# One GpSimd instruction for du * B of two states, and two states in PSUM less often in layer 1

## The chip, the cores and the metric

The kernel runs on one core of one Trainium2 chip. The time is device microseconds from start to end of one execution; the median of three runs before the change is 11,260.47 us (11,260.01 to 11,280.23).

## The reference

Four images of 64 x 64 pixels and 96 channels go through four layers. Layers 0 and 1 are selective scans (layer 0 on the pixels with 192 inner channels, layer 1 on a two-dimensional Fourier transform with 384 inner channels and 64 x 33 positions); layers 2 and 3 are linear attention and a quantized feed-forward block. The change is in the scan that layers 0 and 1 share. Each runs over four directions, with 16 states per channel:

```python
def step(hst, inputs):
    ul, dl, bl, cl = inputs
    dA = jnp.exp(dl[..., None] * A)
    hst = hst * dA + (dl * ul)[..., None] * bl[:, :, None, :]
    y = jnp.einsum('bkdn,bkn->bkd', hst, cl)
    return (hst, y)
```

For every position l, channel d and state n: h = h * exp(delta * A) + (delta * u) * B, and y sums h * C over the 16 states.

## The kernel before

**Phases, segments, steps.** The work has six phases: two for layer 0 (two images each, 64 channels of either side by side on the 128 partitions) and four for layer 1 (an image each). A phase runs through four directions, each cut into segments along the sequence: eight of 512 positions in layer 0, five of 512, 512, 384, 384 and 320 in layer 1. That gives 64 segments in layer 0 and 80 in layer 1. A segment has 12 steps: for each group q of four states (q = 0 to 3), the three chunks c of channels (128 rows each). So there are 768 steps in layer 0 and 960 in layer 1, and each step makes four scans, of states 0 to 3 of its group.

**What a step does on each engine.**
- DVE: four scans along the positions (`scan`, L710). The factor `exp(delta * A)` of states 0 and 1 lies in SBUF (`ax`) and their addend B*du in PSUM, put there by PE's transposes (`transposed`, L678). For states 2 and 3 it is the other way round: the factor lies in PSUM (`ay`), and the addend in the SBUF tile `h`.
- POOL (GpSimd): `front_b` (L700) makes that addend, du * B, for states 2 and 3 of the next step, two instructions into `h[:, 1]` and `h[:, 2]`. `multiply` (L744, L747) saves the last column of the previous step's states and multiplies them by C in place, for the states whose result is in `h`.
- States that are "kept" leave their result in PSUM (`kept_at`). DVE multiplies it by C (`multiply_kept`, L728), ACT saves its last column (`keep_state`, L735). State 0 is kept in every step; state 3 too in some steps, chosen by `self.kept`: every second step in layer 0 (`cfg.KI` is 1), every fourth in layer 1 (`cfg.KI` is 2). In a step with one kept state POOL multiplies three states, in a step with two it multiplies two.
- PE: transposes for the next step, and the sum over states by accumulating transposes into `acc` (`add_rest` and `add_kept`, both by `accumulate`, L757).
- ACT: the exponentials (L682), `make_bx` (L646) and copies.

**Order.** The order on each engine is written out by hand in the loop over `steps`. In step i, PE first accumulates the states of step i-2 (`add_rest(older)`); POOL does `multiply(before)` of step i-1 and then `front_b(nxt)` for step i+1; DVE does scans 0 to 3 of step i with its kept product behind scan 0 and, where state 3 is kept, behind scan 3. The tile `h` has three buffers, so `front_b` for step i+1 writes where step i-2 stood and waits until PE has accumulated that one. PSUM has three banks for the operands of the scans, used in rotation. Other work (projections, transforms, the layers after) runs as generators, `slot` by `slot`, between the steps; GpSimd's part of it are the transposing copies (L335), du itself (L604) and small additions (L1352, L1356).

Of the kernel before, what the change touches and what calls it, by code (L numbers as in the profile page):

```python
# [11 lines left out]
ALU = mybir.AluOpType  # L12
# [10 lines left out]
C, P = 3, 128  # L23
# [7 lines left out]
class Cfg:  # L31
# [5 lines left out]
    def __init__(self, pre, NI, KI, NR, nat, R, parts, rows, segs, eps):  # L37
        self.pre = pre
        self.NI, self.PI, self.KI = NI, P // NI, KI
        self.DI = C * self.PI  # L40
        self.NR, self.L, self.nat = NR, NR * 64, nat
        self.R, self.M = R, R + 2 * NST
        self.parts = parts
        self.rows = [(sum(rows[:i]), n) for i, n in enumerate(rows)]
        self.segs = [(sum(segs[:i]), n) for i, n in enumerate(segs)]
        self.eps = eps
# [466 lines left out]
class Step:  # L513


    def __init__(self, z, q, c):
        self.z, self.q, self.c = z, q, c
        self.nm = f"{z.nm}_{q}_{c}"
        self.kept = (0, 3) if (C * q + c) % (2 * z.cfg.KI) == 1 else (0,)
        self.hk = {}  # L520
        self.px, self.ay = {}, {}


def scans(tc, ctx, phases, ident):
# [8 lines left out]
    nc = tc.nc  # L533
# [161 lines left out]
    def front_b(st):  # L695

        S = st.z.S
        st.h = sp.tile([P, 3, SM], F32, name=f"h_{st.nm}", tag="h", bufs=3)
        for j in range(2):
            nc.gpsimd.tensor_tensor(  # L700
                st.h[:, 1 + j, :S], st.z.du[:, st.c, :S], st.z.b[st.q][:, j, :S], ALU.mult
            )

    def scan(st, j):
        z = st.z
# [93 lines left out]
    with tc.manual_schedule(engines=IN_ORDER):  # L799
# [4 lines left out]
        st = steps[0]  # L804
        for j in range(2):
            transposed(st, j)
        front_x(st)
        front_b(st)
        before = older = None
        more, pgen, pwants, at, due = Pieces(segs[0], 1, 4), none, None, 0, 0.0  # L810
# [32 lines left out]
        for i, st in enumerate(steps):  # L843
            z, q, c, S = st.z, st.q, st.c, st.z.S
# [42 lines left out]
            if nxt:  # L887
                front_b(nxt)
# [734 lines left out]
```

## Time and profile before

The profiled execution took 11,260.07 us, of which 11,258.3 are the span from the first to the last instruction. The mean granted TensorE clock is 0.898. The scan loop runs from 216 to 10,873 us.

| phase | from, us | length, us | steps | us per step |
|---|---|---|---|---|
| layer 0, images 0 and 1 | 216 | 2471 | 384 | 6.44 |
| layer 0, images 2 and 3 | 2687 | 2443 | 384 | 6.36 |
| layer 1, image 0 | 5130 | 1452 | 240 | 6.05 |
| layer 1, image 1 | 6582 | 1415 | 240 | 5.90 |
| layer 1, image 2 | 7997 | 1434 | 240 | 5.97 |
| layer 1, image 3 | 9431 | 1443 | 240 | 6.01 |

The starts are those of each phase's first scan in the timeline. The page's table gives, by engine, busy time and share of the span; rows by line and shape give count, busy time, mean duration, and the idle time of the engine just before, with what ended it. A mean duration of a POOL row includes an overlap of some tens of ns with the next instruction, which start-to-start times in the timeline do not.

### The profile page before, as it was taken

To read this page: it belongs to the slowest core of one execution; us is meant where nothing else is said; L and a number is where in the kernel's file an instruction comes from. 1 tells how busy PE (TensorE), PEld (TensorE's weight loads), DVE (VectorE), ACT (ScalarE), POOL (GpSimd) and SP (SyncE) were. 2 spreads that over 40 slices of the span, in tenths; PEclk is the share of its full clock that TensorE was granted. 3 is DMA by queue.
4 is the path that set the end of the run, shared out by engine and by line. 5 is a ranking of instruction groups with operands and counts; after the bars stand their busy time and mean duration, and the time that the engine had idled before them with its cause. 6 is when DMAs were issued, how large, how long until landed. Compare 5 with 4: busy or idle time off the path is not lost. (4 is left out here: it accounts for less than half of the span.)

```text
span 11258.3 us, 163664 instructions
## 1 busy us (share of the span) xinstructions
PE 9023.4 (80%) x54944; PEld 6618.2 (59%) x54944; DVE 9756.0 (87%) x10419; ACT 9354.2 (83%) x19456; POOL 9614.9 (85%) x7464
## 2 busy tenths in 40 slices
PE   6678788777888888888888888887788777887775
PEld 2555555555667666656665665655556555655554
DVE  6889999889999998999888787988988889789864
ACT  3779999998898998998778788879888888778853
POOL 2999999888998998999789798988989889889860
PEclk8889999888998998999889899998899888899887
DMA  4655554555665556555554444542244322542242
GB/s 146 146 131 128 133 131 120 153 158 143 163 162 134 137 138 144 133 144 161 154 141 131 128 135 137 172 118 92 96 138 143 102 92 98 157 125 96 82 131 40
DMA packets 1205139, 1466.87 MB, mean 130 GB/s; under 512 B 480839, under 2 KB 1017295, under 8 KB 1145799
## 3 DMA queue, kind: packets, MB, share of 16 engines
q1 hardware_dynamic: 1204295, 1456.40, 47.7%
q8 instruction: 434, 7.11, 0.3%
q14 instruction: 410, 3.36, 0.1%
HBM read 1219.66 MB, written 236.50 MB: 129 GB/s over the span
## 5 line engine op out<-in xcount | busy, mean ns | idle before, releaser
L747 POOL TENSOR_TENSOR h_l<-h_l,bc_l 128x1536 f32<-128x1536 f32 (+2 forms) x1728 | 4784.4, 2769 | 192.1 <-DVE h_l L710 73.1
L700 POOL TENSOR_TENSOR h_l<-du_l,bc_l 128x512 f32<-128x512 f32 (+2 forms) x3456 | 3970.4, 1172 | 620.1 <-PE acc_l L757 581.1
L646 ACT ACTIVATE bx_l<-dut_l,bt_l 128x192 f32<-128x192 f32 (+2 forms) x6272 | 2754.6, 499 | 0.3
L757 PE MATMUL acc_l<-ident,h_l 128*128 128x128 f32 (+1 forms) x16656 | 2430.6, 299 | 243.5 <-POOL h_l L747 242.1
L757 PEld LDWEIGHTS acc_l<-ident,h_l 128*128 128x128 f32 (+1 forms) x16656 | 2130.9, 154 | 836.8 <-POOL h_l L747 384.9
L682 ACT ACTIVATE ax_l<-delta_l,l_alog 128x512 f32<-128x512 f32 (+2 forms) x3456 | 2140.7, 667 | 0.0
L710 DVE TENSOR_TENSOR_SCAN h_l<-b_l,state_l,h_l 128x512 f32<-128x512 f32 (+2 forms) x1388 | 1507.6, 1109 | 123.1 <-ACT b_l L682 104.5
L678 PE MATMUL b_l<-ident,bx_l 128*128 128x128 f32 (+1 forms) x6886 | 1215.4, 295 | 210.2 <-DVE h_l L710 203.2
L678 PEld LDWEIGHTS b_l<-ident,bx_l 128*128 128x128 f32 (+1 forms) x6886 | 854.6, 149 | 816.6 <-DVE h_l L710 464.4
L682 ACT ACTIVATE b_l<-delta_l,l_alog 128x512 f32<-128x512 f32 (+2 forms) x1970 | 1232.6, 626 | 117.2 <-DVE h_l L710 49.4
L710 DVE TENSOR_TENSOR_SCAN b_l<-ax_l,state_l,b_l 128x512 f32<-128x512 f32 (+2 forms) x853 | 967.5, 1134 | 254.8 <-PE b_l L678 253.6
L678 PE MATMUL ab_l<-ident,bx_l 128*128 128x128 f32 x5312 | 896.1, 298 | 223.1 <-DVE h_l L710 213.2
L710 DVE TENSOR_TENSOR_SCAN h_l<-ab_l,state_l,h_l 128x512 f32<-128x512 f32 x803 | 992.7, 1261 | 83.2 <-ACT ab_l L682 48.8
L682 ACT ACTIVATE ab_l<-delta_l,l_alog 128x512 f32<-128x512 f32 x1326 | 912.8, 688 | 152.3 <-DVE h_l L710 81.4
L757 PE MATMUL acc_l<-ident,k_l 128*128 128x128 f32 x4760 | 785.8, 293 | 294.8 <-DVE k_l L728 281.6
L710 DVE TENSOR_TENSOR_SCAN h_l<-ax_l,state_l,b_l 128x512 f32<-128x512 f32 (+2 forms) x853 | 963.2, 1129 | 65.0 <-PE b_l L678 62.7
L678 PEld LDWEIGHTS ab_l<-ident,bx_l 128*128 128x128 f32 x5312 | 654.2, 151 | 583.4 <-DVE h_l L710 414.9
L728 DVE TENSOR_TENSOR k_l<-b_l,bc_l 128x512 f32<-128x512 f32 (+2 forms) x1344 | 832.2, 619 | 47.2 <-DMA bc_l<-l_xd_l 1.0
L297 PE MATMUL pc_l<-pad_l,l_dg 128*128 128x512 f32 (+2 forms) x1656 | 788.1, 564 | 59.5 <-ACT uh_l L275 46.8
L757 PE MATMUL acc_l<-ident,hk_l 128*128 128x128 f32 x3628 | 591.8, 297 | 293.7 <-DVE hk_l L728 280.8
L757 PEld LDWEIGHTS acc_l<-ident,k_l 128*128 128x128 f32 x4760 | 582.8, 150 | 390.7 <-DVE k_l L728 317.9
L710 DVE TENSOR_TENSOR_SCAN ab_l<-ax_l,state_l,ab_l 128x512 f32<-128x512 f32 x496 | 631.9, 1274 | 114.5 <-PE ab_l L678 113.8
(252 smaller groups left out, 14452.2 us busy)
## 6 DMA issues: line engine op xcount, KB each, us to landing
bc_l<-l_xd_l SPq DMA_DIRECT2D x640, 512.0 KB
bc_l<-l_xd_l SPq DMA_DIRECT2D x512, 256.0 KB
bc_l<-l_xd_l SPq DMA_DIRECT2D x128, 1024.0 KB
bc_l<-l_xd_l SPq DMA_DIRECT2D x128, 768.0 KB
us_l<-l_u SPq DMA_DIRECT2D x96, 768.0 KB
l_y<-y_l SPq DMA_DIRECT2D x288, 256.0 KB
yt_l<-l_y SPq DMA_DIRECT2D x264, 192.0 KB
yt_l<-l_y SPq DMA_DIRECT2D x128, 384.0 KB
```

What stands on the lines that cost most here:

```text
L297: nc.tensor.matmul(pc[:, : n * 64].rearrange("p (r w) -> p r w", w=64), diag[:, t, :], pad[:, r - p0 + dy : r - p0 + dy + n, dx : dx + 64] ...
L646: nc.scalar.activation(t[:n, b, :, ch], z.dut[:n, b, :, ch], AF.Copy, scale=z.bt[:n, b, m : m + 1])
L678: nc.tensor.transpose(pb[:, t : t + n], st.z.bx[st.q, j][:n, b, st.c], ident[:n, :n])
L682: nc.scalar.activation(out, z.delta[:, st.c, : z.S], AF.Exp, scale=z.blk.A[:, st.c, z.k, n : n + 1])
L700: nc.gpsimd.tensor_tensor(st.h[:, 1 + j, :S], st.z.du[:, st.c, :S], st.z.b[st.q][:, j, :S], ALU.mult)
L710: nc.vector.tensor_tensor_scan(h[:, ::step], a[:, ::step], b[:, ::step], 0.0 if z.first else z.state[st.c][:, n : n + 1], ALU.mult, ALU.add,)
L728: nc.vector.tensor_tensor(hk[:, : z.S], kept_at(st, j), z.c[st.q][:, j, : z.S], ALU.mult)
L747: nc.gpsimd.tensor_tensor(h, h, z.c[st.q][:, 1 : 1 + m, : z.S], ALU.mult)
L757: nc.tensor.matmul(z.acc[st.c][:m, b, :], hc[:, t : t + m], ident, start=(first and b == 0), stop=(last and b == 0), is_transpose=True,)
```

## The change

Two edits. In `front_b` the loop over the two states becomes one `tensor_tensor` over a 2 x S pattern: B of both states is the first operand, and du of the chunk, repeated over the two states by a stride of 0, the second. The values are the same. In `Step`, layer 1 (where `cfg.KI` is 2) keeps state 3 in PSUM in every sixth step of a segment, steps 1 and 7 of 12, where it was steps 1, 5 and 9. Layer 0's rule stays at every second step.

```diff
-        self.kept = (0, 3) if (C * q + c) % (2 * z.cfg.KI) == 1 else (0,)
+        self.kept = (0, 3) if (C * q + c) % (2 if z.cfg.KI == 1 else 6) == 1 else (0,)
...
-        for j in range(2):
-            nc.gpsimd.tensor_tensor(
-                st.h[:, 1 + j, :S], st.z.du[:, st.c, :S], st.z.b[st.q][:, j, :S], ALU.mult
-            )
+        nc.gpsimd.tensor_tensor(
+            st.h[:, 1:, :S],
+            st.z.b[st.q][:, :, :S],
+            st.z.du[:, st.c : st.c + 1, :S].to_broadcast([P, 2, S]),
+            ALU.mult,
+        )
```

## The prediction

> **What bounds the kernel now.** The page's table of engines comes first: no engine is full, four are near it.
>
> ```profile
> span 11258.3 us, 163664 instructions
> ...
> PE 9023.4 (80%) x54944; PEld 6618.2 (59%) x54944; DVE 9756.0 (87%) x10419; ACT 9354.2 (83%) x19456; POOL 9614.9 (85%) x7464
> ```
>
> The chain of waits does not help here: it adds up to some 5% of the span and starts with the last product at 10,873 us, so it covers only the tail. The scan loop before it has to be read by stages. From the timeline I took where each of the six phases' first scan starts, and asked for busy time between these points. Columns: stretch, its length, then busy us and count of PE, PE's weight loads, DVE, ACT, POOL, then clock and DMA.
>
> ```profile
> 216.00:2687.00 2471.00, 1898.48 (x10843) 1350.67 (x10844) 2250.66 (x2148) 2201.16 (x4702) 2311.68 (x1711) 0.91 0.54 136
> 2687.00:5130.00 2443.00, 2025.92 (x12859) 1562.59 (x12857) 2271.86 (x2202) 2220.51 (x4767) 2260.70 (x1658) 0.92 0.59 146
> 5130.00:6582.00 1452.00, 1271.21 (x7802) 946.20 (x7802) 1201.78 (x1348) 1145.53 (x2236) 1238.03 (x1010) 0.90 0.49 142
> 7997.00:9431.00 1434.00, 1142.77 (x7224) 842.74 (x7223) 1283.02 (x1479) 1221.44 (x2514) 1263.63 (x1014) 0.89 0.38 113
> ```
>
> POOL is the fullest engine in the first phase (2311.68/2471 = 94%), DVE in the second (93%), PE in layer 1's first image (88%, its ends modelled), DVE in its third (89%). POOL and DVE lie within 3% of each other in all of them. In equal slices, 560 to 1700 us has POOL at 97% and hardly a wait in it; that is the only stretch where one engine is plainly the bound.
>
> Who waits for whom, over the whole run (engine, instruction, releaser: us, times, longest):
>
> ```profile
> POOL h_l L700 <- PE acc_l L757: 581.1, 336, 7.7
> DVE b_l L710 <- PE b_l L678: 313.6, 254, 6.5
> PE acc_l L757 <- POOL h_l L747: 242.1, 167, 9.2
> DVE h_l L710 <- POOL h_l L700: 54.8, 50, 8.4
> ```
>
> The four lines close a ring. PE's accumulation of step i-2 (add_rest) waits for POOL's product; behind it in PE's queue stand the transposes that DVE's next scans need; and POOL's du * B waits for the same accumulation to release the buffer h. POOL itself waits for PE in 336 of 1728 steps, so in those POOL is ahead and a shorter POOL instruction buys nothing there.
>
> **What the Trainium skill says.** "GPSIMD Engine Reference", section 3.1 (Elementwise), puts a GpSimd tensor_tensor at about 2.6 cycles per element plus a dispatch per instruction. The trace agrees in kind: from the rows below, (3454-2366)/512 = 2.125 ns an element and 2366-1024*2.125 = 190 ns fixed. "Perfetto Trace Analysis", section GPSIMD Engine Instruction, advises start-to-start spacing and not durations; here that matters, see below. "SBUF — State Buffer", section Who interferes with whom, says that a DVE instruction with two SBUF inputs blocks against a GpSimd one that reads SBUF. All four scans and L728 have one operand in PSUM, before and after, and the 128x512 scans take 1259 to 1274 ns whether they write PSUM or SBUF; so I cost a longer POOL instruction at no contention.
>
> ```profile
> L700 POOL TENSOR_TENSOR h_l<-du_l,bc_l 128x512 f32<-128x512 f32 x2304 | 2892.8, 1279 | 309.9 <-PE acc_l L757 293.1 <-issue 14.5 <-POOL h_l L747 1.4
> L747 POOL TENSOR_TENSOR h_l<-h_l,bc_l 128x1536 f32<-128x1536 f32 x672 | 2320.8, 3454 | 81.5 <-DVE h_l L710 33.6 <-DVE qb L1174 3.2
> L747 POOL TENSOR_TENSOR h_l<-h_l,bc_l 128x1024 f32<-128x1024 f32 x480 | 1135.8, 2366 | 39.5 <-DVE h_l L710 6.9
> ```
>
> **The change part by part.** *Merging L700.* By durations a pair costs 2*1279 = 2558 and one instruction of 1024 elements 2366: 192 ns less. But consecutive POOL instructions overlap, as POOL's timeline shows:
>
> ```profile
> 5156.19 2.53 POOL L700 TENSOR_TENSOR h_l<-du_l,bc_l 128x512 f32<-128x512 f32 x2
> 5158.64 0.21 POOL L744 COPY state_l<-h_l 128x3 f32<-128x3 f32 x1
> 5158.93 3.45 POOL L747 TENSOR_TENSOR h_l<-h_l,bc_l 128x1536 f32<-128x1536 f32 x1
> 5162.34 2.50 POOL L700 TENSOR_TENSOR h_l<-du_l,bc_l 128x512 f32<-128x512 f32 x2
> 5164.79 0.18 POOL L744 COPY state_l<-h_l 128x2 f32<-128x2 f32 x1
> 5165.05 2.36 POOL L747 TENSOR_TENSOR h_l<-h_l,bc_l 128x1024 f32<-128x1024 f32 x1
> 5167.37 2.51 POOL L700 TENSOR_TENSOR h_l<-du_l,bc_l 128x512 f32<-128x512 f32 x2
> ```
>
> Start to start the pair takes 5158.64-5156.19 = 2.45 and the 1024-wide product 5167.37-5165.05 = 2.32. The mean over all places without a gap is 2.455 against 2.321 (512), 1.906 against 1.775 (384), 1.637 against 1.505 (320): 0.133 us a step. Layer 0 has 768 steps: 102 us; layer 1 has 960: 128 us. Unknown is the stride-0 operand. L1352, which has one, takes 922 ns for 384 elements and L1356 beside it without one 916, so no penalty; both are shorter than the 1004 of L700 at 384, but both read 16-bit data. Bounds for one merged instruction: 2.455 (nothing gained, loss excluded since two passes do the same) and, if the stride-0 operand were the reason for 922, about 0.19+1024*(0.922-0.19)/384 = 2.14. I take 2.32.
>
> *Layer 1's kept steps.* Two states in PSUM happen in 2 of 12 steps of a segment in place of 3: with 80 segments, 80 steps change. In these POOL multiplies 3 states in place of 2. Start to start that is 3.408-2.321 = 1.087 (512), 2.590-1.775 = 0.815 (384), 2.184-1.505 = 0.679 (320). The five segments of a pass (512, 512, 384, 384, 320) sum to 4.48, times 16 passes: POOL +72 us. DVE loses the L728 of state 3. In gapless DVE steps of the timeline one with it lasts 6.16 and one without 5.43 at 512; 4.87 and 4.28 at 384; 4.12 and 3.57 at 320: 0.73, 0.59, 0.55, sum 3.19, times 16: DVE -51 us. ACT loses 80 state copies (L735) of 0.147 at most, 12 us. PE's matmuls keep their number. The PSUM bank of state 3 is free one L728 sooner.
>
> So POOL: -102 in layer 0, -128+72 = -56 in layer 1. DVE: -51, all in layer 1.
>
> *The wait that is added.* Scan 2 needs half of du * B and scan 3 the other; now scan 2 needs the whole. Behind it on DVE stand scan 3 and the next step's scans, behind those PE's transposes. I paired the k-th two L700 with the k-th four scans of the timeline: the first half ends 3.5 us before scan 2 in the median, yet in 161 of 1728 steps scan 2 starts before or less than 0.14 us after the second half ends. Counted up to 0.1 us after it, the shortfalls add up to 120 us: 44 in layer 0, 76 in layer 1. They come in 57 clusters of neighbouring steps; the largest of each, which is what DVE loses if it only shifts once per cluster, add up to 51. POOL arrives 0.133 us sooner for each step since its last idle moment, about 4 steps (some 430 idle moments in 1728 steps), 0.5 us; mean shortfall is 0.79. So I take 20 us of delay, of which half is caught up in DVE's later waits for PE: +10.
>
> *What of the savings reaches the end.* Phase 1: the 560 to 1700 stretch holds 1140/6.435 = 177 steps, POOL-bound: 177*0.133 = 24. The other 207 steps save 27; PE or DVE wait for POOL in part of them; a third: 9. Phase 2: PE waits for POOL's product there 8.8 us and DVE 3.3 in all; of 51 saved I take 6; DVE is late next. Layer 1: POOL -14 and DVE -13 an image, about 1% of each; when both partners of the ring shrink, PE and ACT (82% and 83% busy over its four images) are next, so I take 70% of the smaller: 9 an image, 36. Sum: -24-9-6-36+10 = -65. The profiled execution's own time is 11260.07, the median 11260.47: the sum gives 11,195 against either.
>
> **The rivals.** *POOL is the bound throughout*: all 102+56 = 158 us arrive, 11,102. For: POOL has the largest share in two of the six phases and lies within 3% of the largest in the others, and PE waits 242 us for its products. Against: the 581 us that POOL waits. *Hidden*: POOL's gain only lengthens its waits for PE, and scan 2's delays eat what DVE gives up, -51+51: 11,260, within 22. For: phase 2's few waits on POOL. Against: the 97% stretch, where nothing can hide it. *Slower*: scan 2 is the place; its shortfalls pass in full, +120, against 33 in phase 1 and DVE's 51: +36, 11,296. The longer run of steps between relieved ones in layer 1 (five in place of three, each with POOL at 3.41+2.32+0.26 = 5.99 against DVE's 5.43 at 512) feeds it: POOL falls behind by 2.8 us there in place of 3*(6.12-5.43) = 2.1. It decides from (33+51)/120 = 70% of the shortfalls on. Against: DVE waits for L700 only 50 times now.
>
> **How the numbers follow.** Below 0.2%, 22 us, a measurement of this kernel can't tell a gain from none. Forecast, a part arrives: 0.50. All arrives: 0.20. Hidden: 0.14. Slower: 0.16. Faster is 0.70 and a little of the hidden case: 0.71; same 0.14; slower 0.15. The range goes from the all-arrives case, with a little for a merged instruction under 2.32, 11,090, to within the slower case, 11,282.
>
> **What would show it.** L700 must appear 1728 times, 2.36 us at 1024 elements; POOL busy near 9614.9-158 = 9457, DVE near 9705. The first phase should shorten by about 33 us, the second by under 15, each image by about 9 less its share of the delays. If DVE's waits for L700 grow from 54.8 to well above 100 us, the slower rival is at work; if L700 lasts 2.5, merging gave nothing; if phase 2 shortens by 40 or more, POOL was the bound where I took DVE.

## The result, and the profile after

The changed kernel takes 11,227.00 us in the median of five runs (11,204.68 to 11,235.58), beside 11,274.52 us for the kernel before (five runs): the ratio is 0.9955, with a 95% interval of 0.9944 to 0.9965. That is 51 us of 11,274.52 by the ratio, where the forecast of 11,195 meant 65. The profiled execution took 11,227.0 us, 33 less than the one of before.

The page of the changed kernel, its span and its table of engines:

```profile
span 11225.2 us, 160774 instructions
...
PE 9045.2 (81%) x54944; PEld 6633.9 (59%) x54944; DVE 9704.5 (86%) x10339; ACT 9343.7 (83%) x19392; POOL 9443.0 (84%) x5736
```

POOL has 9614.9 - 9443.0 = 172 us less to do (forecast 158) and DVE 51 less (forecast 51), and 1728 instructions are gone from POOL. The span is 33 us shorter. So the work went away as it should, and most of the time did not follow.

POOL's two rows of 1024 elements, by line and shape: du * B of two states with its stride-0 operand (L699), and the product of two states with C without one (L749; two lines were added above it).

```profile
L699 POOL TENSOR_TENSOR h_l<-bc_l,du_l 128x1024 f32<-128x1024 f32 x1152 | 2724.8, 2365 | 338.9 <-PE acc_l L759 319.8 <-issue 9.6 <-DVE h_l L712 6.1
L749 POOL TENSOR_TENSOR h_l<-h_l,bc_l 128x1024 f32<-128x1024 f32 x448 | 1059.2, 2364 | 35.9 <-DVE h_l L712 5.1
```

They last the same to 1 ns: the stride-0 operand costs nothing. Start to start, as POOL's timeline has it:

```profile
5164.26 2.37 POOL L749 TENSOR_TENSOR h_l<-h_l,bc_l 128x1024 f32<-128x1024 f32 x1
5166.58 2.39 POOL L699 TENSOR_TENSOR h_l<-bc_l,du_l 128x1024 f32<-128x1024 f32 x1
5168.90 0.19 POOL L746 COPY state_l<-h_l 128x3 f32<-128x3 f32 x1
```

Over all places without a gap the merged instruction takes 2.312 us where the pair took 2.455; 1.764 for 1.906 at 384 columns; 1.495 for 1.637 at 320. That is 0.142 us a step, where 0.133 was forecast.

Busy time by phase in the changed kernel (the same four phases, columns as before):

```profile
217.00:2678.00 2461.00, 1894.58 (x10844) 1344.80 (x10845) 2247.64 (x2148) 2201.61 (x4702) 2258.66 (x1329) 0.90 0.55 136
2678.00:5114.00 2436.00, 2033.30 (x12853) 1568.98 (x12852) 2271.26 (x2202) 2220.27 (x4767) 2207.42 (x1273) 0.92 0.60 146
5114.00:6567.00 1453.00, 1279.17 (x7809) 949.43 (x7807) 1190.88 (x1329) 1144.34 (x2221) 1222.32 (x771) 0.89 0.49 142
7974.00:9404.00 1430.00, 1154.86 (x7215) 855.44 (x7213) 1269.85 (x1458) 1217.30 (x2497) 1245.72 (x774) 0.89 0.38 114
```

By the first scans of the phases in the two timelines, the phases changed by -10.2, -6.8, +0.4, -8.2, -3.1 and -7.4 us, -35 in all. That is less than the 51 of the ratio, mostly because the profiled execution of the kernel before (11,260.07 us) was as fast as the fastest of its five. Phases of the same code differ between the traces of this document by some 5 us in layer 0 and by up to 10 in an image of layer 1, so single phases are known no better. POOL fell by 53 in each of the first two phases (2311.68 to 2258.66, 2260.70 to 2207.42) and got a fifth and an eighth of that back as time.

Who waits for whom:

```profile
POOL h_l L699 <- PE acc_l L759: 617.3, 367, 7.2
DVE b_l L712 <- PE b_l L678: 305.5, 252, 5.0
POOL state_l L746 <- DVE h_l L712: 270.4, 209, 10.7
PE acc_l L759 <- POOL h_l L749: 171.1, 135, 9.8
DVE h_l L712 <- POOL h_l L699: 80.0, 86, 10.1
```

These lines show where the rest went. POOL's waits for PE rose from 581.1 to 617.3 and those for DVE, ahead of the state copy, from 205.5 to 270.4: 101 us that POOL now spends waiting. PE waits less for POOL's products (242.1 to 171.1), but DVE's largest wait, for PE's transposes, nearly stays (313.6 to 305.5; the profile lists the same wait under other tile names too, and all of them add up to 578.9 before and 566.5 after), and DVE waits for du * B 86 times in place of 50.

### The profile page after: what moved, and what is told of

The parts are those of the page before. It is cut to its first block, busy times and chain, and to the rows that moved or that the text cites. A ratio compares the mean times of both kernels' runs of the same rounds, so it can differ in the third digit from the quotient of the medians.

```text
span 11225.2 us, 160774 instructions
## 1 busy us (share of the span) xinstructions
PE 9045.2 (81%) x54944; PEld 6633.9 (59%) x54944; DVE 9704.5 (86%) x10339; ACT 9343.7 (83%) x19392; POOL 9443.0 (84%) x5736
## 5 line engine op out<-in xcount | busy, mean ns | idle before, releaser
L749 POOL TENSOR_TENSOR h_l<-h_l,bc_l 128x1536 f32<-128x1536 f32 (+2 forms) x1728 | 4853.3, 2809 | 208.1 <-DVE h_l L712 64.8
L699 POOL TENSOR_TENSOR h_l<-bc_l,du_l 128x1024 f32<-128x1024 f32 (+2 forms) x1728 | 3718.5, 2152 | 669.2 <-PE acc_l L759 617.3
L759 PEld LDWEIGHTS acc_l<-ident,h_l 128*128 128x128 f32 (+1 forms) x16928 | 2184.2, 155 | 760.0 <-issue 343.0
L759 PE MATMUL acc_l<-ident,h_l 128*128 128x128 f32 (+1 forms) x16928 | 2483.6, 300 | 172.8 <-POOL h_l L749 171.1
L712 DVE TENSOR_TENSOR_SCAN h_l<-ab_l,state_l,h_l 128x512 f32<-128x512 f32 x849 | 1048.9, 1262 | 95.9 <-ACT ab_l L682 49.0
L759 PE MATMUL acc_l<-ident,k_l 128*128 128x128 f32 (+1 forms) x4580 | 759.7, 293 | 283.3 <-DVE k_l L730 270.3
L730 DVE TENSOR_TENSOR k_l<-b_l,bc_l 128x512 f32<-128x512 f32 (+2 forms) x1291 | 800.8, 620 | 44.3
L759 PEld LDWEIGHTS acc_l<-ident,k_l 128*128 128x128 f32 (+1 forms) x4580 | 560.2, 150 | 377.3 <-DVE k_l L730 304.6
```

What stands on the lines that cost most here:

```text
L699: nc.gpsimd.tensor_tensor(st.h[:, 1:, :S], st.z.b[st.q][:, :, :S], st.z.du[:, st.c : st.c + 1, :S].to_broadcast([P, 2, S]), ALU.mult,)
L712: nc.vector.tensor_tensor_scan(h[:, ::step], a[:, ::step], b[:, ::step], 0.0 if z.first else z.state[st.c][:, n : n + 1], ALU.mult, ALU.add,)
L730: nc.vector.tensor_tensor(hk[:, : z.S], kept_at(st, j), z.c[st.q][:, j, : z.S], ALU.mult)
L749: nc.gpsimd.tensor_tensor(h, h, z.c[st.q][:, 1 : 1 + m, : z.S], ALU.mult)
L759: nc.tensor.matmul(z.acc[st.c][:m, b, :], hc[:, t : t + m], ident, start=(first and b == 0), stop=(last and b == 0), is_transpose=True,)
```

## The experiments

Each ratio is against the kernel before on the same chip, with its 95% interval.

**The two edits apart.** The merge alone:

```diff
-        self.kept = (0, 3) if (C * q + c) % (2 if z.cfg.KI == 1 else 6) == 1 else (0,)
+        self.kept = (0, 3) if (C * q + c) % (2 * z.cfg.KI) == 1 else (0,)
```

> The merge alone; layer 1 keeps state 3 every fourth step as before. My theory (both parts bring a share): the merge gives layer 0's whole gain, 17 us by the phase starts of the two traces, and of layer 1 some 10, so ratio near 0.9975 (-28 us). Rival A, the merge does it all: ratio 0.9955. Rival B, the gain is DVE's relief in layer 1 and the merge is hidden by the wait it adds: ratio 0.999 or more.

Measured: 0.9968 (0.9957 to 0.9979), -36 us. POOL's busy time is 9373.0, 242 us less than before. In its trace DVE waits 15 us more for du * B than the 54.8 of before:

```profile
DVE h_l L712 <- POOL h_l L699: 70.0, 63, 10.4
```

So some of what POOL saves is waited for at scan 2.

The kept rule alone, the first hunk of the change's diff, with the pair of instructions as before:

> The kept rule alone (two of 12 steps in layer 1 have two states in PSUM), du * B in two instructions. My theory: DVE loses 51 us, POOL gains 72 in layer 1; about -10 us, ratio 0.999, layer 0 unchanged. Rival A (POOL is the bound of layer 1): slower by 20 to 70 us, ratio 1.002 to 1.006. Rival B (DVE is the bound of layer 1): faster by 30 to 50, ratio 0.996.

Measured: 1.0005 (0.9996 to 1.0013). DVE's busy time fell to 9713.3, 43 less, POOL's rose to 9678.6, 64 more, and the time stood still. So the kept rule on its own brings nothing that can be measured; the merge brings most of the gain, and may bring all of it, since its interval and the change's (0.9944 to 0.9965) overlap.

**The kept rule carried further**, in the changed kernel:

```diff
-        ... % (2 if z.cfg.KI == 1 else 6) == 1
+        ... % (2 if z.cfg.KI == 1 else 12) == 1
```

> The changed kernel with layer 1 keeping state 3 in one step of twelve (step 1 alone): POOL +72 and DVE -51 us against the change, the same again as the change's own second edit. Theory: the exchange of POOL for DVE time is neutral over a wide range, ratio 0.9955 within 0.0015. Rival: layer 1 is tipped to POOL, +20 to +50 us, ratio 0.9975 to 1.000. Rival: DVE is the bound of layer 1, -20 or more, ratio 0.9935.

Measured: 0.9967 (0.9954 to 0.9979). With three, two or one kept step of twelve the merged kernel stands at 0.9968, 0.9955 and 0.9967: no difference is shown. The exchange of some 50 us of DVE for some 70 of POOL is neutral over that range, as far as intervals of some 14 us to either side can tell.

**The added wait alone.** The kernel before with its two instructions in the other order:

```diff
-        for j in range(2):
+        for j in (1, 0):
             nc.gpsimd.tensor_tensor(
```

> The kernel before with the two du * B instructions in the other order, the second state first: POOL's work is unchanged, but scan 2 now waits for both, as it does after the merge. It prices the added wait alone. The prediction's +10 us, at most +20 (before its catching up): ratio 1.001 to 1.002. The slower rival: the 120 us of shortfalls pass in the main, ratio 1.007 to 1.011. No cost at all: 1.000.

Measured: 1.0006 (0.9998 to 1.0014), +7 us with an interval from -2 to +16. DVE's waits of this kind doubled all the same:

```profile
DVE h_l L710 <- POOL h_l L700: 108.4, 93, 10.4
```

From 54.8 us in 50 waits to 108.4 in 93, that is 54 us of added waiting, of which 7 reach the end (16 at the most). The delay of scan 2 is in the main caught up in what DVE would have waited for anyway: as far as one trace of each tells, its waits for PE's transposes, over all tile names, are 32 us shorter for it (547.0, and 578.9 before). The slower rival is out.

**The saving alone.** The kernel before with POOL's product shortened by as much as the merge saves; it leaves the last 21 or 32 columns of h unmultiplied by C:

```diff
-        nc.gpsimd.tensor_tensor(h, h, z.c[st.q][:, 1 : 1 + m, : z.S], ALU.mult)
+        n = z.S - (21 if m == 3 else 32)
+        nc.gpsimd.tensor_tensor(h[:, :, :n], h[:, :, :n], z.c[st.q][:, 1 : 1 + m, :n], ALU.mult)
```

> The kernel before with POOL's product h * C cut by 63 elements a step (the last 21 columns of three states, or 32 of two, are left unmultiplied), which saves the same 0.133 us of POOL a step as the merge, without the wait on both halves. If the added wait eats a part of the merge's gain, this is faster than the merge alone by that part: ratio 0.9965 where the merge alone has 0.9975. If POOL's time is hidden whatever the wait, both are near 0.999. If POOL were the bound, -230 us, ratio 0.980.

Measured: 0.9944 (0.9931 to 0.9956), -63 us for 258 us less of POOL (9356.6). DVE's waits for du * B in it:

```profile
DVE h_l L710 <- POOL h_l L700: 32.8, 27, 8.0
```

They fell from 54.8 to 32.8, where the merge raises them. The merge alone has 0.9968 for nearly the same saving: 27 us lie between the two, in intervals that all but touch. In the traces the spans differ by 22 us and DVE's waits for du * B by 37 (70.0 against 32.8), so the added wait on the whole instruction is the likely place of it. But the run with the other order puts that wait at 7 us, with 16 at the most. There is a rival that no run separates from it: the shortened product also ends sooner itself, and PE waits for it (147.6 us in the merge alone, 128.0 here). So what the added wait costs stays open.

**Four times that saving**, 84 or 126 columns left out:

> As the run with the shortened product, four times as much: POOL's h * C leaves out the last 84 columns of three states or 126 of two, 0.535 us a step, 925 us in all. If each us of POOL's work is worth what the first was (67 us of time for 230 of work), -250 us, ratio 0.978. If the first cut took most of what POOL holds up and DVE and ACT are next, -90 to -130 us, ratio 0.988 to 0.992.

Measured: 0.9903 (0.9889 to 0.9916), -110 us for 933 us less of POOL (8681.7). The first 258 us of POOL brought 63, the next 675 only some 46. Saved in this way, POOL's time is worth about a quarter of itself at first and soon less than a tenth.

**The stretch that was taken for POOL-bound.** Steps 52 to 233 fill it in each of these kernels; before, after, and with the fourfold shortened product, they last as follows (length, then PE, weight loads, DVE, ACT, POOL):

```profile
570.50:1703.50 1133.00, 891.76 (x5239) 637.65 (x5238) 1057.95 (x1015) 1019.05 (x2200) 1101.66 (x812) 0.93 0.52 131
```

```profile
569.50:1702.50 1133.00, 893.56 (x5238) 639.00 (x5236) 1057.82 (x1014) 1019.08 (x2200) 1076.58 (x628) 0.93 0.53 131
```

```profile
548.00:1671.50 1123.50, 897.04 (x5239) 640.18 (x5238) 1056.77 (x1015) 1018.32 (x2200) 1005.49 (x814) 0.93 0.53 132
```

POOL loses 25 us and the length does not move; it loses 96 and the length falls by 10. Other kernels with the same layer 0 show how far one trace can be trusted: without the merge the same steps take 1137.1 us (kept rule alone), with it 1129.7 (merge alone) and 1131.8 (one kept step of twelve). So the merge gave between 0 and 7 us here. The shortened product, with 26 us less of POOL than before, takes 1127.1. POOL at 97% was not the bound.

DVE is busy for 1057 to 1058 us in each of the three, so the length can change only with DVE's waits. These are the waits for POOL in the stretch, before and after:

```profile
PE acc_l L757 <- POOL h_l L747: 51.7, 27, 7.0
DVE h_l L710 <- POOL h_l L700: 11.8, 8, 3.9
```

```profile
PE acc_l L759 <- POOL h_l L749: 33.7, 16, 5.8
DVE h_l L712 <- POOL h_l L699: 16.0, 11, 3.8
```

PE waits 18 us less for POOL's products, but this does not come through to DVE, whose largest wait for transposes in the stretch stays (12.7 and 12.2 us), and DVE waits 4 us more for du * B.

**DVE relieved with POOL out of the way.** The fourfold shortened product, and layer 0 with a second kept state every third step in place of every second:

```diff
-        ... % (2 * z.cfg.KI) == 1
+        ... % (3 if z.cfg.KI == 1 else 4) == 1
```

> The fourfold shortened product (columns of h * C left out, as before) with layer 0 keeping state 3 in every third step in place of every second: POOL has room, so DVE's 128 saved products of 0.73 us (93 us, 22 of them from 560 to 1700 us) show what DVE's time is worth once POOL is out of the way. If DVE is then the bound of layer 0: -60 to -90 us against the fourfold shortened one, ratio 0.982 to 0.985, and 15 to 22 us of it from 560 to 1700 us. If ACT or the waits through PE are the bound: -20 or less, ratio 0.9885 or above.

Measured: 0.9883 (0.9870 to 0.9897), so some 22 us under the fourfold shortened one for 79 us less of DVE (9742.8 to 9664.2). The same 182 steps:

```profile
552.50:1664.50 1112.00, 895.48 (x5241) 641.31 (x5240) 1036.38 (x984) 1011.22 (x2173) 1036.87 (x813) 0.93 0.54 133
```

In this stretch DVE lost 20 us and the length 11.5: about half is passed on here, and about a quarter over the run, where the intervals of the two kernels overlap. The result lies at the edge of the second case: with POOL out of the way, a part of DVE's time comes back in this stretch, but in the run as a whole no engine's time comes back in full.

**The same relief in the changed kernel**, layer 0 at every third step and layer 1 at every sixth:

> The changed kernel with layer 0 keeping state 3 in every third step in place of every second: 128 of 768 steps change, DVE -93 us (0.73 each), POOL +139 (1.087 each). If DVE is the bound of layer 0, another -20 to -40 us, ratio 0.992 to 0.9935. If layer 0 answers to POOL, as the run with a shortened product suggests (28 of its 67 us came in layer 0), +10 to +40, ratio 0.9965 to 0.999.

Measured: 0.9946 (0.9933 to 0.9958), POOL 9573.9 and DVE 9627.0 us. That lies between the two cases of the expectation. It has the lowest median of the kernels that compute everything (11,212.54 us) and beats the kernel before; against the change's 0.9955 the intervals overlap, so that it beats that too is not shown. Steps 52 to 233 in it:

```profile
570.50:1702.00 1131.50, 902.57 (x5231) 646.21 (x5231) 1037.89 (x983) 1012.88 (x2173) 1105.45 (x627) 0.92 0.53 131
```

DVE is down by the same 20 us as in the run before this one, but POOL is back at 1105, and the length is that of the change; DVE's waits for du * B here are 31.9 us in place of 16.0. So less of DVE alone brings nothing in this stretch, less of POOL alone at most some 10 us, and less of both 21: the two bound it together.

**Whether the ring through PE holds POOL back.** A fourth buffer of h, with one buffer fewer for y and for xs:

```diff
-        st.h = sp.tile([P, 3, SM], F32, name=f"h_{st.nm}", tag="h", bufs=3)
+        st.h = sp.tile([P, 3, SM], F32, name=f"h_{st.nm}", tag="h", bufs=4)
...
-        y = sp.tile([P, NBK, P], F32, name=f"y_{st.nm}", tag="y", bufs=2)
+        y = sp.tile([P, NBK, P], F32, name=f"y_{st.nm}", tag="y", bufs=1)
```

> The changed kernel with four buffers of h in place of three (to make room, one buffer in place of two for y and for xs, used once a chunk and once a segment). POOL need not wait for PE's sum of step i-2 before du * B of step i+1. If the added wait of scan 2 and the ring through PE are what eats the merge's gain, POOL's 617 us of waiting for PE shrink to under 200, scan 2's 80 us of waiting to under 30, and the ratio goes to 0.990 to 0.993. If POOL's wait is only slack of an engine that is ahead, the ratio stays at the change's 0.9955 within 0.0015.

Measured: 1.0155 (1.0141 to 1.0169), which neither theory had. The room was taken from the wrong place:

```profile
ACT y_l L790 <- DMA l_y<-y_l: 335.1, 100, 10.5
```

ACT stood still until y's only buffer was written out, and the exponentials stood behind it (DVE's waits for them are 450.7 us, 264.2 in the change). The run says nothing on h. With y at two buffers again and the room from xs and bt:

```diff
-        xs = sp.tile([P, SM], F32, name=f"xs_{nm}", tag="xs", bufs=2)
+        xs = sp.tile([P, SM], F32, name=f"xs_{nm}", tag="xs", bufs=1)
...
-        z.bt = sp.tile([P, NBK, rows], F32, name=f"bt_{nm}", tag=f"bt{cfg.pre}", bufs=2)
+        z.bt = sp.tile([P, NBK, 76], F32, name=f"bt_{nm}", tag="bt", bufs=2)
```

> The changed kernel with four buffers of h in place of three; the room comes from one buffer of xs in place of two (used once a segment) and from one tag for both layers' bt, with y at two buffers as in the change. The first run with four buffers had 335 us of ACT waiting for the write-out of y, which hid what it asked. If the ring through PE (POOL waits for PE's sum before du * B) eats the merge's gain: ratio 0.990 to 0.993, POOL's wait for PE under 200 us. If that wait is slack of an engine ahead: 0.9955 within 0.0015, and the wait turns up again before the state copy, as a wait for DVE.

Measured: 0.9966 (0.9954 to 0.9977). POOL's waiting in it:

```profile
POOL state_l L746 <- DVE h_l L712: 765.9, 449, 10.7
POOL h_l L749 <- DVE h_l L712: 168.6, 83, 6.8
```

The 617 us of waiting for PE are gone from the list (0.8 us are left), and the waiting for DVE is up from 270.4 to 765.9 and from 64.8 to 168.6. The time is no better. As far as this run tells, the wait was the slack of an engine that is ahead. It doesn't exclude that the room taken from xs and bt cost what the fourth buffer gained: beside the change its trace is 8 us longer in the first phase, 14 longer in layer 1's first image and 15 shorter in its last. No wait speaks for such a cost, though; ACT waits as long before xs as in the change (16.6 and 16.5 us).

**du * B first on POOL**, on top of the four buffers:

```diff
+            if nxt:
+                front_b(nxt)
             if before:
                 multiply(before)
-            if nxt:
-                front_b(nxt)
```

> The run with four buffers of h and room from xs and bt, with du * B of the next step issued on POOL ahead of the product of the step before, so that scan 2 finds it 2 to 3 us sooner and its wait goes. If the added wait is what separates the merge (0.9968) from the shortened product (0.9944), ratio 0.993 to 0.9945 and scan 2's waits for du * B under 20 us. Rival: the product, and with it PE's sum and the transposes behind it, comes 2.3 us later and costs more than the wait did: ratio 0.998 or above, PE's waits for POOL's product well above 171 us.

Measured: 0.9969 (0.9957 to 0.9981), between the two cases.

```profile
DVE b_l L712 <- PE b_l L678: 333.3, 261, 6.4
DVE ab_l L712 <- PE ab_l L678: 201.6, 122, 6.8
PE acc_l L759 <- POOL h_l L749: 278.5, 182, 9.3
...
DVE h_l L712 <- POOL h_l L699: 5.1, 3, 2.5
```

With four buffers alone these four are 293.6, 159.7, 158.3 and 72.6 us. Scan 2's wait is gone, 5.1 us in 3 waits, and PE's wait for the products has grown by 120 in return; behind it DVE waits 82 us longer for the transposes. One wait of DVE was exchanged for another, and the time stayed where four buffers alone had it.

**POOL's state copy on ACT.** In the changed kernel the saving of the last columns left `multiply` and became an ACT copy:

```diff
             front_y(st, 2)
+            if before:
+                keep_rest(before)
...
-            nc.gpsimd.tensor_copy(
+            nc.scalar.copy(
```

> The changed kernel with the copy of the last columns of h (POOL, 1392 times, 0.26 us start to start, 360 us of POOL) given to ACT, early in the next step, and POOL's product waiting for it. If POOL's time is worth what the shortened products showed (-63 for 230 us, -110 for 925), some -60 us against the change, ratio 0.990, less what ACT's 200 us more cost. If ACT, 83% busy and with the exponentials in the same queue, is as near the bound as POOL: 0.9955 or slower, up to 1.005.

Measured: 0.9985 (0.9977 to 0.9992), slower than the change. POOL fell to 9208.0 us, but:

```profile
POOL h_l L753 <- ACT state_l L744: 961.7, 689, 11.9
```

POOL's product now waits for ACT 689 times. A part of this only stands where other waits stood (POOL's for PE fall from 617.3 to 200.3 us, and the 270.4 for DVE ahead of the copy are gone), but PE's waits for POOL's product rise from 171.1 to 229.5. Work taken from an engine in exchange for a wait on another engine's queue was no gain here.

## Why the prediction was right

**Its sign and its mechanism held.** The merge takes time off POOL, a part of it arrives, the second edit roughly balances itself. The measured -51 us lies near the forecast -65, but the sum is no proof of its terms. By the interval of the ratio the gain is 39 to 63 us. The forecast lies just outside of that; with nothing for the term that was most wrong (below), it would have been 41, just inside.

**The costs of the instructions held.** Merged duration 2365 ns against 2366; POOL's and DVE's busy time within 14 and 1 us of the numbers given. That DVE's fits to 1 us is in part luck: the kept rule alone took 43 us off DVE, not 51, and added 64 to POOL, not 72. Neither bound for the unknown, the stride-0 operand, was needed. Two counts were off without consequence: the stretch from 560 to 1700 us holds 183 steps and not 177, as its steps are shorter than the phase's mean, and the kept rule takes 64 state copies off ACT and not 80 (19,456 to 19,392 instructions), since the last segment of a pass saves none.

**The term that was mis-sized is the POOL-bound stretch.** The prediction said of 560 to 1700 us that it "is the only stretch where one engine is plainly the bound" and took 24 us for it. It gave 0 (1133.0 and 1133.0; 7 at the most, by the other kernels), and even 96 us less of POOL gave 10. An engine that is 97% busy with hardly a wait was read as the one that sets the pace. DVE at 93% in the same steps bounds them with it: its 1058 us stayed the same while POOL's fell, and the length fell by 21 us where both were cut, but by some 10 at most where one was. In such a pair the fuller engine has less slack; cutting it alone makes slack (POOL's waits for DVE ahead of the copy rise from 7.7 to 23.1 us in this stretch) and little time. The first phase as a whole gave 10 where 33 were forecast, and nearly all of it came outside the stretch: its other 202 steps went from 1338.2 to 1327.8 us, where the prediction took 9 for them.

**The second phase** gave 7 where 6 were forecast: with few waits for POOL (PE 8.8, DVE 3.3 us), little was to be had. With the fourfold shortened product it gave 6 (2442.6 to 2436.8), so the reading of the waits held here.

**Layer 1** gave 18 in the trace of the change where 36 were forecast, but 34 in the run with layer 0 at every third step, whose layer 1 is the same code. So this term is not shown to be wrong. Its reason is not shown to be right either: the forecast took 70% of the smaller of what POOL and DVE lose in an image, because both have less to do. Kept rules of three, two and one in twelve come out alike, so DVE's 51 us are paid for with POOL's 72, as a trade, and the merge alone, which leaves DVE its work, shortened the four images by 18 us too.

**The added wait** was put at +10 us after its catching up. The other order measured +7 (-2 to +16); the comparison of the merge with the shortened product would put it at up to 27. The slower rival needed 70% of the 120 us of shortfalls to pass. The other order added 54 us of waits, and its time says that about an eighth of that passed, three tenths at the most. In the change DVE's waits for du * B grew to 80.0 us, short of the 100 that the prediction named as the sign of this rival.

**The rivals.** POOL as the bound throughout, 11,102, is out: the change got 51 of the 158 us, and even a fourfold cut got only 110. The hidden case is out by the interval. What stays open is what sets the pace when neither POOL nor DVE does. DVE's waits for PE's transposes, over all tile names, are 578.9 us before and 566.5, 543.9, 543.7 and 542.7 with the change, the merge alone and the two shortened products. They stay the largest wait of DVE, and the fourfold cut of POOL takes no more off them than the first. Whether the first cut shortened them at all is not clear, as they are 547.0 with the other order, which cuts no work, and 596.6 with the kept rule alone. No run here cut PE's work, so that PE's queue is the third bound was not shown; nor was it for ACT, for whose exponentials DVE waits 241.9 us before and 264.2 with the change.

## What to carry to other kernels

Where four engines lie within a few per cent of each other, a cut of one of them returns a fraction: here a quarter of the first 258 us that a shortened product took off POOL and less than a tenth of the next 675, and some 15% of the merge's 242. Price such a cut by the waits for that engine in that stage, not by its busy share, even at 97%, and follow these waits to the next fullest engine: in the stretch shown PE waited 51.7 us for POOL, but DVE only 11.8. Before buying time on one engine with work, or with a wait, on another, or room for a buffer from another tile, look at what stands behind the new wait: of the trades tried here none gained a measurable amount over the change.

## What the runs showed of the hardware that was not expected

A GpSimd product with one operand repeated by a stride of 0 takes 2365 ns for 1024 elements and one without 2364; start to start it is a little shorter, 2.312 against 2.321 us. Consecutive GpSimd instructions overlap by some 50 ns in the profile (a 2365 ns instruction every 2.31 us), so two merged into one save 0.142 us and not the 0.192 that their durations suggest.
